# Six-channel feature groups of a tanh-attention kernel: 64 partitions of one block, or 32 partitions of two blocks

## The chip, the cores and the metric

One core of a Trainium2 chip runs the whole program. The metric is device time in microseconds; the kernel before takes 6139.32 us (median of three runs, 6136.94 to 6142.77).

## What is computed

The input x has 8 images of 128 channels and 36 x 36 positions. The reference applies a convolution layer with its own attention, and then, on each image's 1296 tokens of 128 channels, an additive (tanh) attention and a mixture-of-experts layer. The change concerns the tanh attention:

```python
q = jnp.einsum('bld,ed->ble', x, Wq) + bq
k = jnp.einsum('bld,ed->ble', x, Wk) + bk
t = jnp.tanh(q[:, :, None, :] + k[:, None, :, :])
scores = jnp.einsum('bijd,d->bij', t, w) + bw[0]
attn = jax.nn.softmax(scores, axis=-1)
return jnp.einsum('bij,bjd->bid', attn, x)
```

The term t has 8 x 1296 x 1296 x 128 elements. Everything around it runs once per image (group norm, 3 x 3 convolutions, a 1156-key softmax attention; then the gate, top 8 of 1296 tokens for each of 64 experts, two expert matmuls).

## The kernel before

**How tanh becomes matmuls.** A weighted sum of tanh over a small group of channels is one quotient. With a pattern s of signs for the group's channels, the sum of w tanh(q + k) is N / D, where D adds exp(s.q) exp(s.k) over all patterns, and N adds the same products, each times c_s = s.w. Both are inner products over patterns, so a matmul that contracts over the patterns gives N or D for a tile of 128 keys by 432 queries. A group of five channels has 32 patterns and a group of six has 64. The 128 channels are 16 groups of five (80 channels) and 8 groups of six (48).

**Feature blocks.** The patterns of all groups fill NF = 8 blocks of 128 partitions: blocks 0 to 3 hold four groups of five each, 32 partitions a group; blocks 4 to 7 hold two groups of six each, 64 partitions a group. The sign matrix is built by `signs` (lines 522 to 537) with GpSimd's affine selects. From it come the key features `kf` (128 partitions, 8 blocks, 128 keys; made once per image by `keys`, stored in HBM, fetched by `prefetch`) and the query features `qf` (one tile per block: part 0 is exp, for D; part 1 is part 0 times c_s, for N; made by `query_block`: a matmul, an ACT exponential, a GpSimd multiply). All data are float32, and each float32 matmul stands in the trace as two loads and two matmuls.

**Loops.** For each of the 8 images, three chunks of 432 queries; for each chunk, 11 tiles of keys, ten of 128 and one of the last 16. A pair of chunk and key tile is a unit. A unit of 128 keys has 12 slots (line 49), in each of which two groups are worked on, h = 0 and 1, each in a PSUM bank of its own. The slots go in rounds of three: two groups of five in one half (64 partitions) of a block, two in the other half, then the two groups of six of a block. The half that is taken first alternates from round to round. The unit of the last 16 keys has two slots, with 32 columns of output per group and four groups in a bank (lines 65 to 67, 952 to 955). There are 240 units of 12 slots and 24 of two: 2928 slots.

**A slot on the engines** (main loop, lines 1113 to 1146). For slot p, TensorE computes n, the numerators of slot p (`numerators`, into the pool `ps_n` of four banks), and d, the denominators of slot p + 3 (`denominators`, LAG = 3, into the pool `ps_d`, two buffers of two banks). ACT takes the logarithm of d (line 972), and every second slot exponentiates the negative of two slots' logarithms (line 975), which gives 1 / D. DVE multiplies n by it. In the rounds' first two slots the products go to `rp` (line 1003) and GpSimd adds them up (lines 1010, 1012). In the third slots (k = 2, 5, 8, 11, DVE_PAIRS) DVE multiplies in PSUM and adds to `accd` itself: two multiplies at line 997 and two adds at line 999; at k = 2, the unit's first, it multiplies one half straight into `accd` at line 992, then lines 993 and 994.

**Side work.** The next image's convolutions and attention, its keys, the weighted sums of the finished chunk and the gate are generators in four lanes. After a slot's own work, `matmul_turn` (line 1077) lets them put one burst of matmuls on TensorE, paced by a balance that is counted when the program is built, not in DVE_PAIRS' preceding slots except for the lane `first_of_all`. Their PSUM tiles come from the same four banks as n. `take_turns` (line 1072) lets them issue the other engines' work. Everything is issued in the order in which it is written (a manual schedule); each engine takes its own instructions in that order.

**Query blocks of the next chunk.** `qf` has nine buffers for eight blocks. In a chunk's last unit, a block of the next chunk is made when one of the present chunk's is no longer needed; IN_TURN gives the order of blocks, and lines 1136 to 1141 choose the slots.

Of the kernel before, what the change touches and what calls it, by code (L numbers as in the profile page):

```python
# [3 lines left out]

# [6 lines left out]
F32 = mybir.dt.float32  # L11
# [9 lines left out]
CH = 432  # L21
# [24 lines left out]
NF = 8  # L46
# [1 line left out]

SLOTS = []
for m in range(NF // 2):  # L50
    for i in range(2):
        half = (m + i) % 2
        SLOTS.append((m, [slice(64 * half + 32 * h, 64 * half + 32 * h + 32) for h in range(2)]))
    SLOTS.append((NF // 2 + m, [slice(64 * h, 64 * h + 64) for h in range(2)]))
NP = len(SLOTS)
IN_TURN = [m + i for m in range(NF // 2) for i in (0, NF // 2)]
LAG = 3
SHIFT = 6.5
DVE_PAIRS = (2, 5, 8, 11)
# [2 lines left out]


HALVES = [slice(0, 64), slice(64, 128)]
REM_BANKS = [[(q + i, rows) for i in range(2) for rows in HALVES] for q in (0, 2)]
REM_BANKS.append([(NF // 2 + i, slice(0, 128)) for i in range(4)])
REM_SLOTS = [REM_BANKS[:2], REM_BANKS[2:]]


@with_exitstack  # L70
def kernel(
# [58 lines left out]
    with ExitStack() as loop, ExitStack() as score:  # L130
# [82 lines left out]
            pattern=[[C // G, G], [0, C // G]], channel_multiplier=-1,  # L213
        )

        pairs = const.tile([128, 2, 2], F32, tag="pairs", name="pairs")
        nc.gpsimd.memset(pairs, 0.0)
        for s in range(2):
            nc.gpsimd.memset(pairs[64 * s : 64 * s + 64, 1, s : s + 1], 1.0)
            for o in (32 * s, 64 + 32 * s):  # L220
                nc.gpsimd.memset(pairs[o : o + 32, 0, s : s + 1], 1.0)

        by_key = const.tile([128, 2, REM], F32, tag="by_key", name="by_key")
        for s in range(2):
# [297 lines left out]
        def signs():  # L522

            sign = big_tile("sign")[:, : NF * 128]
            nc.gpsimd.memset(sign, 0.0)
            for n, first, half in ((5, 0, sign[:, : NF * 64]), (6, FIVES, sign[:, NF * 64 :])):
                groups = NF * 64 >> n
                for r in range(n):
                    v = half.rearrange("p (g h b l) -> p g h b l", g=groups, b=2, l=2**r)
                    for bit, value in ((0, -1.0), (1, 1.0)):  # L530
                        w = v[:, :, :, bit, :]
                        nc.gpsimd.affine_select(
                            out=w, in_=w, compare_op=ALU.not_equal, fill=value, base=-first - r,
                            pattern=[[-n, groups], [0, 2 ** (n - 1 - r)], [0, 2**r]],
                            channel_multiplier=1,
                        )
            return sign

        feat = {}
# [127 lines left out]
        def keys(b, tiles):  # L667

            xT = prepared[b][1]
            yield matmuls(1)  # L670
            for t in tiles:
                o, n = KT[t]
                first = (b, t) == (0, order[0])
                if first:
                    kf_of[0] = kfp.tile([128, NF, 128], F32, tag="kf", name="kf")
                for q0 in (0, NF // 2):
                    some = slice(q0, q0 + NF // 2)
                    pk = aux("pk1").rearrange("p (q t) -> p q t", t=128)
                    for q in range(NF // 2):
                        bmm(pk[:, q, :n], a_k[:, (q0 + q) * 128 : (q0 + q + 1) * 128],  # L680
                           xT[:, o : o + n], start=True, stop=True)
                    yield TAKE
                    if first:
                        ks = kf_of[0][:, some, :]
                    else:
                        ks = kstp.tile([128, NF // 2, 128], F32, tag="ks", name="ks")
                    nc.scalar.activation(ks[:, :, :n], pk[:, :, :n], AF.Exp)
                    kd3 = kd[b][t].rearrange("p (q t) -> p q t", t=128)[:, some, :]
                    if n == REM:

                        for x in range(2):
                            nc.gpsimd.tensor_scalar(
                                ks[:, :, (x + 1) * n : (x + 2) * n], ks[:, :, :n],
                                pairs[:, min(q0, 1), x : x + 1], None, ALU.mult,
                            )
                        nc.sync.dma_start(kd3[:, :, : 2 * n], ks[:, :, n : 3 * n])
                    else:
                        nc.sync.dma_start(kd3, ks)
                    if q0 > 0:
                        made.add((b, t))  # L700
                    yield matmuls()
# [209 lines left out]
        def drain(*gens):  # L911
            for g in gens:
                for _ in g:
                    pass
# [22 lines left out]
        def new_block(b, c, q):  # L937
            qf = qfp.tile([128, 2, CH], F32, tag="qf", name="qf")
            qf_of[b, c, q] = qf
            return query_block(b, c, q, qf)  # L940

        def products(u, k, part, outs):

            b, c, j = units[u]
            kf = kf_of[u]
            if j < NKT - 1:
                q, rows = SLOTS[k]
                for h in range(2):
                    mm(outs[h][:, :CH], kf[rows[h], q, :], qf_of[b, c, q][rows[h], part, :],  # L949
                       start=True, stop=True)  # L950
                return
            for out, bank in zip(outs, REM_SLOTS[k]):
                for i, (q, rows) in enumerate(bank):
                    mm(out[32 * i : 32 * i + 32, :CH], kf[rows, q, :32],  # L954
                       qf_of[b, c, q][rows, part, :], start=True, stop=True)

        def banks(u, k):
            return 2 if units[u][2] < NKT - 1 else len(REM_SLOTS[k])

        def denominators(p):  # L960

            if p >= len(slots):
                return
            u, k = slots[p]
            d = ps_d.tile([128, 2, 512], F32, tag="d", name="d")
            n = banks(u, k)
            products(u, k, 0, [d[:, h, :] for h in range(n)])
            if k % 2 == 0:
                lq_of[u, k // 2] = lp.tile([128, 4, CH], F32, tag="lq", name="lq")
            lq = lq_of[u, k // 2]  # L970
            o = 2 * (k % 2)
            nc.scalar.activation(lq[:, o : o + n, :], d[:, :n, :CH], AF.Ln)  # L972
            if k % 2 == 1:
                some = lq[:, : o + n, :]
                nc.scalar.activation(some, some, AF.Exp, scale=-1.0)  # L975

        def numerators(p):
            ns = [ps_n.tile([128, 512], F32, tag="n", name="n") for _ in range(banks(*slots[p]))]
            products(*slots[p], 1, ns)
            return [ps[:, :CH] for ps in ns]  # L980

        def terms(p, ns):

# [116 lines left out]
        a_q, a_k, cs_s, fb_s, eb_s = (feat[n] for n in ("a_q", "a_k", "cs_s", "fb_s", "eb_s"))  # L1100
        drain(tokens(0), keys(0, order[:1]))
        for i, q in enumerate(IN_TURN):
            if i < 3:
                drain(new_block(0, 0, q))
            else:
                first_of_all.append(new_block(0, 0, q))
        for p in range(LAG):
            denominators(p)
        drain(keys(0, order[1:3]))
        prefetch(1)  # L1110
        urgent.append(keys(0, order[3:]))
# [1 line left out]
        for p, (u, k) in enumerate(slots):  # L1113
            b, c, j = units[u]
            rem = j == NKT - 1
            if k == 0:
                prefetch(u + 2)
                if c == 0 and j == 1:
                    if b > 0:
                        gates.append(gating(b - 1))  # L1120
                    if b == NB - 1:
                        gates.append(residuals(4))
                    if b + 1 < NB:
                        background.extend(
                            (normal(b + 1), conv_keys(b + 1), layer0(b + 1), tokens(b + 1),
                             keys(b + 1, range(NKT)))
                        )
            take_turns(p, k)
            ns = numerators(p)
            denominators(p + LAG)  # L1130
            terms(p, ns)
            if pending and pending[0][0] <= p:
                exps(p, *pending.popleft()[1:])
            last = p + 1 == len(slots) or slots[p + 1][0] != u

            if j == order[-1] and u + 1 < len(units) and k % 3:
                used = IN_TURN.index(SLOTS[k][0]) + 1
                if used < NF:
                    first_of_all.append(new_block(*units[u + 1][:2], IN_TURN[used]))
            elif j == order[-2] and last and u + 2 < len(units):  # L1140
                first_of_all.append(new_block(*units[u + 2][:2], IN_TURN[0]))
            matmul_turn(p, k)
            if last and rem:
                first_of_all.append(rem_scores(p, u, live.pop("rem")))
            elif last:
                pending.append((p + 7, u, sums(u)))
# [211 lines left out]
```

The softmax here doesn't subtract the row's maximum and nothing guards it: scores larger than these inputs give would overflow.

## Time and profile before

| | |
|---|---|
| median of the runs | 6139.32 us |
| profiled execution, its span | 6139.0 us |
| mean granted TensorE clock | 0.985 of full speed |
| ACT busy between 400 and 6000 us | 5020 us of 5600 |
| DVE busy between 400 and 6000 us | 4509 us of 5600 |
| numerator matmuls, L949, 32 rows | 7680 instructions, 571 ns |
| numerator matmuls, L949, 64 rows | 3840 instructions, 580 ns |
| denominator matmuls, L949, 32 rows | 7680 instructions, 575 ns |
| denominator matmuls, L949, 64 rows | 3840 instructions, 534 ns |
| last-key matmuls, L954, 64 rows | 384 + 384 instructions, 528 ns |
| last-key matmuls, L954, 128 rows | 192 + 192 instructions, 538 ns |
| ACT logarithm, L972 | 2904 of 881 ns, 24 shorter |
| ACT exponential, L975 | 1440 of 1644 ns, 24 shorter |
| DVE multiply to rp, L1003 | 3912 of 600 ns |
| DVE multiply in PSUM, L997 | 1440 of 608 ns |
| DVE add to accd, L999 | 1440 of 602 ns |

The profile is of one execution, and its rows are groups of like instructions: line, engine, how often, mean time of one. PE is TensorE's matmuls, PEld its weight loads, which overlap them. "32*128" is a matmul with 32 rows of contraction and 128 columns of output. Matmuls overlap and their ends are modelled, so their busy times can't be added up to a span; the starts in the timeline tell more. An idle time is followed by "<-" and the instruction that ended it.

### The profile page before, as it was taken

Reading aid. Unit: us, or ns where it says so; the run is one execution under the profiler, and the core shown is the slowest. Engines: PE = TensorE matmul, PEld = TensorE weight load, DVE = VectorE, ACT = ScalarE, POOL = GpSimd, SP = SyncE. Lnnn points to the kernel's source line nnn. Section 1 sums busy time; section 2 is a strip of 40 time slices with the busy share of each in tenths; the row PEclk is TensorE's granted clock in tenths of the full one; section 3 lists DMA queues with packets and bytes.
Section 4 is the critical chain, followed back from the end, with each engine's and each line's share of the span. In section 5 each row is a group of like instructions: output and inputs, shape, how many; then the busy total and the mean of one; then the engine's idle time right before and its main releaser. Section 6 shows DMA issues by size and latency. Waiting matters only on the chain.

```text
span 6139.0 us, 93072 instructions
## 1 busy us (share of the span) xinstructions
PE 5957.9 (97%) x33480; PEld 2862.1 (47%) x33480; DVE 4796.4 (78%) x9521; ACT 5279.9 (86%) x5371; POOL 4597.7 (75%) x2819
## 2 busy tenths in 40 slices
PE   7999999999999999999999999999999999999996
PEld 5454444544544445444455444454444544544443
DVE  4787878877788787877888777887778877788882
ACT  1888898888988888889998889888898888999990
POOL 4777777777787777778778786877777777787870
PEclk9999999999999999999999999999999999999997
DMA  1210011100110002100111001110011100110008
GB/s 44 70 37 22 25 62 38 34 25 28 68 43 20 26 27 71 39 24 23 44 55 39 22 24 59 44 39 22 20 65 40 34 25 28 58 50 29 28 20 297
DMA packets 151519, 270.87 MB, mean 44 GB/s; under 512 B 45648, under 2 KB 76752, under 8 KB 151056
## 3 DMA queue, kind: packets, MB, share of 16 engines
q1 hardware_dynamic: 151056, 264.92, 13.0%
q8 instruction: 264, 4.33, 0.3%
q14 instruction: 199, 1.63, 0.1%
HBM read 200.41 MB, written 64.19 MB: 43 GB/s over the span
## 4 chain that ended last, share of the span: by engine, by line
PE 77%; ACT 7%; DVE 6%; issue 6%; POOL 2%; DMA 1%; SPq 0%; DVEq 0%; POOLq 0%; ACTq 0%
PE n L949 37%; PE d L949 12%; PE pa L284 7%; PE pc L284 5%; ACT lq L972 5%; PE s L284 3%; PE pk L284 3%; PE pq L284 3%; DVE rp L1003 2%; DVE n L997 1%; DVE accd L999 1%; PE d L954 1%; ACT lq L975 1%; DMA w<-in_weight_dram 1%; PE n L954 1%
## 5 line engine op out<-in xcount | busy, mean ns | idle before, releaser
L1012 POOL TENSOR_TENSOR accp<-accp,rp 128x864 f32<-128x864 f32 x1440 | 2915.8, 2025 | 1041.0 <-DVE rp L1003 948.8
L949 PE MATMUL n<-qf,kf 32*128 32x432 f32 (+1 forms) x11520 | 3325.3, 574 | 46.5 <-ACT e L1032 13.3
L949 PE MATMUL d<-qf,kf 32*128 32x432 f32 (+1 forms) x11520 | 2991.6, 561 | 38.7 <-ACT lq L972 38.2
L972 ACT ACTIVATE lq<-d 128x864 f32<-128x864 f32 x2928 | 2524.2, 878 | 542.6 <-PE d L949 512.1
L1003 DVE TENSOR_TENSOR rp<-n,lq 128x432 f32<-128x432 f32 x3912 | 2173.3, 600 | 743.5 <-PE d L949 542.8
L975 ACT ACTIVATE lq<-lq 128x1728 f32<-128x1728 f32 (+1 forms) x1464 | 2398.2, 1638 | 46.3
L949 PEld LDWEIGHTS n<-qf,kf 32*128 32x128 f32 (+1 forms) x11520 | 1206.4, 184 | 1600.3 <-DVE rp L1003 581.5
L949 PEld LDWEIGHTS d<-qf,kf 32*128 32x128 f32 (+1 forms) x11520 | 1090.0, 185 | 422.1 <-issue 224.7
L997 DVE TENSOR_TENSOR n<-n,lq 128x432 f32<-128x432 f32 x1440 | 814.9, 608 | 142.1 <-PE n L949 88.5
L999 DVE TENSOR_TENSOR accd<-n,accd 128x432 f32<-128x432 f32 x1440 | 866.3, 602 | 24.6
L1010 POOL TENSOR_TENSOR accp<-rp 128x864 f32<-128x864 f32 x240 | 485.2, 2022 | 197.7 <-DVE rp L1003 195.6
L711 POOL TENSOR_SCALAR qf<-qf,cs_s 128x432 f32<-128x432 f32 x192 | 260.9, 1365 | 45.0 <-ACT qf L710 44.4
L284 PEld LDWEIGHTS pa<-xh,e 128*108 128x108 f32 x1920 | 222.5, 174 | 131.1 <-DVE rp L1003 56.0
L1021 POOL TENSOR_TENSOR accd<-accp,accd 128x432 f32<-128x432 f32 x240 | 265.2, 1105 | 18.8
L1019 POOL TENSOR_TENSOR accp<-accp 128x432 f32<-128x432 f32 x240 | 264.4, 1102 | 16.7
L284 PE MATMUL pa<-xh,e 128*108 128x129 f32 x1920 | 262.9, 283 | 8.7 <-ACT e L1032 5.2
L284 PE MATMUL s<-q,k 128*116 128x432 f32 x480 | 230.3, 568 | 1.7 <-DVE q L316 1.4
L284 PEld LDWEIGHTS pk<-xT,a_k 128*128 128x128 f32 x1408 | 171.2, 192 | 107.0 <-DVE n L997 33.7
L462 POOL TENSOR_TENSOR tot<-tot,e 116x432 f32<-116x432 f32 x192 | 212.0, 1104 | 6.0 <-ACT e L471 4.6
L471 ACT ACTIVATE e<-s 116x432 f32<-116x432 f32 x240 | 124.9, 520 | 98.3 <-PE s L284 97.9
L284 PE MATMUL pa<-e,vw 116*128 116x432 f32 x480 | 204.6, 549 | 0.0
L284 PE MATMUL pk<-xT,a_k 128*128 128x128 f32 (+1 forms) x1408 | 202.5, 287 | 0.1
(213 smaller groups left out, 3788.4 us busy)
## 6 DMA issues: line engine op xcount, KB each, us to landing
kf<-kd SPq DMA_DIRECT2D x239, 512.0 KB
kd<-ks SPq DMA_DIRECT2D x158, 256.0 KB
w<-in_weight_dram SPq DMA_DIRECT2D x32, 1024.0 KB
wk_t<-wk_t_d SPq DMA_DIRECT2D x7, 768.0 KB
wv_t<-wv_t_d SPq DMA_DIRECT2D x7, 768.0 KB
wq_t<-wq_t_d SPq DMA_DIRECT2D x7, 768.0 KB
x<-in_x_dram SPq DMA_DIRECT2D x8, 648.0 KB
t<-tokd SPq DMA_DIRECT2D x96, 54.0 KB
```

The source lines that it names most:

```text
L284: mm(out, lhsT, rhs, **kw)
L711: nc.gpsimd.tensor_scalar(qf[:, 1, :], qf[:, 0, :], cs_s[:, q : q + 1], None, ALU.mult)
L949: mm(outs[h][:, :CH], kf[rows[h], q, :], qf_of[b, c, q][rows[h], part, :], start=True, stop=True)
L972: nc.scalar.activation(lq[:, o : o + n, :], d[:, :n, :CH], AF.Ln)
L975: nc.scalar.activation(some, some, AF.Exp, scale=-1.0)
L997: mult(ns[h], ns[h], lq[:, o + h, :])
L999: nc.vector.tensor_add(live["d"], ns[h], live["d"])
L1003: mult(rp[:, h, :], n, lq[:, o + h, :])
L1010: nc.gpsimd.tensor_add(live["p"], live["r"], rp)
L1012: nc.gpsimd.tensor_add(live["p"], live["p"], rp)
L1019: nc.gpsimd.tensor_add(s[:, 0, :], s[:, 0, :], s[:, 1, :])
L1021: nc.gpsimd.tensor_add(d, s[:, 0, :], d)
```

## The change

The groups of six are laid out anew. Their 64 patterns no longer stand on 64 partitions of one block: the 32 patterns of the first five signs stand on 32 partitions of block 4 or 5 with the sixth sign negative, and on the same partitions of block 6 or 7 with the sixth sign positive. A block of 4 to 7 so holds 32 patterns of four groups. A slot of groups of six takes, for each of its two groups, two 32-row matmuls, over block 4 + m // 2 and block 6 + m // 2, which accumulate in the group's PSUM bank; all slots now work on one half of the partitions, and the half alternates from slot to slot.

`products` becomes a generator that yields after each block, and `in_rounds` takes turns between the numerators of slot p and the denominators of slot p + 3: n and d of the first block, then n and d of the second. For groups of five this leaves the order of issue as it was. The slots of the last 16 keys take eight accumulating 64-row matmuls where they had four of 128 rows. The order of the query blocks and the slots at which the next chunk's are made (NEXT_AT) follow the new order of use; four of the first chunk's blocks, not three, are made ahead of the loop. `signs` has 32 affine selects where it had 22, and `pairs`, the mask for the last keys' features, loses the form for 64 partitions.

```diff
 for m in range(NF // 2):
-    for i in range(2):
-        half = (m + i) % 2
-        SLOTS.append((m, [slice(64 * half + 32 * h, 64 * half + 32 * h + 32) for h in range(2)]))
-    SLOTS.append((NF // 2 + m, [slice(64 * h, 64 * h + 64) for h in range(2)]))
+    for blocks, half in (
+        ((m,), m % 2),
+        ((m,), (m + 1) % 2),
+        ((NF // 2 + m // 2, NF // 2 + 2 + m // 2), m % 2),
+    ):
+        rows = [slice(64 * half + 32 * h, 64 * half + 32 * h + 32) for h in range(2)]
+        SLOTS.append((blocks, rows))
-IN_TURN = [m + i for m in range(NF // 2) for i in (0, NF // 2)]
+IN_TURN = [0, 4, 6, 1, 2, 3, 5, 7]
+NEXT_AT = {1: 4, 5: 6, 6: 1, 7: 2, 8: 3, 10: 5, 11: 7}
...
-REM_BANKS = [[(q + i, rows) for i in range(2) for rows in HALVES] for q in (0, 2)]
-REM_BANKS.append([(NF // 2 + i, slice(0, 128)) for i in range(4)])
+REM_BANKS = [[((q + i,), rows) for i in range(2) for rows in HALVES] for q in (0, 2)]
+REM_BANKS.append([
+    ((NF // 2 + m, NF // 2 + 2 + m), rows) for m in range(2) for rows in HALVES
+])
...
-            for n, first, half in ((5, 0, sign[:, : NF * 64]), (6, FIVES, sign[:, NF * 64 :])):
-                groups = NF * 64 >> n
-                for r in range(n):
...
+            for n, first, groups, top in ((5, 0, 16, None), (6, FIVES, 8, -1.0), (6, FIVES, 8, 1.0)):
+                part = sign[:, at - NF * 64 : at - NF * 64 + groups * 32]
+                at += groups * 32
+                for r in range(5):
...
+                if top is not None:
+                    filled(part.rearrange("p (g l) -> p g l", g=groups), top, first + 5,
+                           [[-n, groups], [0, 32]])
...
-                q, rows = SLOTS[k]
-                for h in range(2):
-                    mm(outs[h][:, :CH], kf[rows[h], q, :], qf_of[b, c, q][rows[h], part, :],
-                       start=True, stop=True)
+                blocks, rows = SLOTS[k]
+                for q in blocks:
+                    for h in range(2):
+                        mm(outs[h][:, :CH], kf[rows[h], q, :],
+                           qf_of[b, c, q][rows[h], part, :],
+                           start=(q == blocks[0]), stop=(q == blocks[-1]))
+                    yield
                 return
             for out, bank in zip(outs, REM_SLOTS[k]):
-                for i, (q, rows) in enumerate(bank):
-                    mm(out[32 * i : 32 * i + 32, :CH], kf[rows, q, :32],
-                       qf_of[b, c, q][rows, part, :], start=True, stop=True)
+                for i, (blocks, rows) in enumerate(bank):
+                    for q in blocks:
+                        mm(out[32 * i : 32 * i + 32, :CH], kf[rows, q, :32],
+                           qf_of[b, c, q][rows, part, :],
+                           start=(q == blocks[0]), stop=(q == blocks[-1]))
+            yield
...
+        def in_rounds(*gens):
+            for _ in zip_longest(*gens):
+                pass
...
-            if i < 3:
+            if i < 4:
                 drain(new_block(0, 0, q))
...
-            ns = numerators(p)
-            denominators(p + LAG)
-            terms(p, ns)
+            ns = []
+            in_rounds(numerators(p, ns), denominators(p + LAG))
+            terms(p, [ps[:, :CH] for ps in ns])
...
-            if j == order[-1] and u + 1 < len(units) and k % 3:
-                used = IN_TURN.index(SLOTS[k][0]) + 1
-                if used < NF:
-                    first_of_all.append(new_block(*units[u + 1][:2], IN_TURN[used]))
+            if j == order[-1] and u + 1 < len(units) and k in NEXT_AT:
+                first_of_all.append(new_block(*units[u + 1][:2], NEXT_AT[k]))
```

More of the change, by code (lines that the diff above doesn't have):

```diff
@@ L2 @@
 from contextlib import ExitStack
-from itertools import chain
+from itertools import chain, zip_longest
 import concourse.bass as bass
@@ L214 @@
         )
-        pairs = const.tile([128, 2, 2], F32, tag="pairs", name="pairs")
+        pairs = const.tile([128, 2], F32, tag="pairs", name="pairs")
         nc.gpsimd.memset(pairs, 0.0)
         for s in range(2):
-            nc.gpsimd.memset(pairs[64 * s : 64 * s + 64, 1, s : s + 1], 1.0)
             for o in (32 * s, 64 + 32 * s):
-                nc.gpsimd.memset(pairs[o : o + 32, 0, s : s + 1], 1.0)
+                nc.gpsimd.memset(pairs[o : o + 32, s : s + 1], 1.0)
         by_key = const.tile([128, 2, REM], F32, tag="by_key", name="by_key")
@@ L525, in signs, with filled @@
             nc.gpsimd.memset(sign, 0.0)
-            for n, first, half in ((5, 0, sign[:, : NF * 64]), (6, FIVES, sign[:, NF * 64 :])):
-                groups = NF * 64 >> n
-                for r in range(n):
-                    v = half.rearrange("p (g h b l) -> p g h b l", g=groups, b=2, l=2**r)
-                    for bit, value in ((0, -1.0), (1, 1.0)):
[L531 to L536, printed above, removed]
+            def filled(w, value, first, pattern):
+                nc.gpsimd.affine_select(
+                    out=w, in_=w, compare_op=ALU.not_equal, fill=value, base=-first,
+                    pattern=pattern, channel_multiplier=1,
+                )
+            at = NF * 64
+            for n, first, groups, top in ((5, 0, 16, None), (6, FIVES, 8, -1.0), (6, FIVES, 8, 1.0)):
+                part = sign[:, at - NF * 64 : at - NF * 64 + groups * 32]
+                at += groups * 32
+                for r in range(5):
+                    v = part.rearrange("p (g h b l) -> p g h b l", g=groups, b=2, l=2**r)
+                    for bit, value in ((0, -1.0), (1, 1.0)):
+                        filled(v[:, :, :, bit, :], value, first + r,
+                               [[-n, groups], [0, 2 ** (4 - r)], [0, 2**r]])
+                if top is not None:
+                    filled(part.rearrange("p (g l) -> p g l", g=groups), top, first + 5,
+                           [[-n, groups], [0, 32]])
             return sign
@@ L693, in keys @@
                                 ks[:, :, (x + 1) * n : (x + 2) * n], ks[:, :, :n],
-                                pairs[:, min(q0, 1), x : x + 1], None, ALU.mult,
+                                pairs[:, x : x + 1], None, ALU.mult,
                             )
@@ L966, in denominators @@
             n = banks(u, k)
-            products(u, k, 0, [d[:, h, :] for h in range(n)])
+            yield from products(u, k, 0, [d[:, h, :] for h in range(n)])
             if k % 2 == 0:
@@ L975, in denominators, with numerators @@
                 nc.scalar.activation(some, some, AF.Exp, scale=-1.0)
[L977 to L980, printed above, removed]
+        def numerators(p, ns):
+            for _ in range(banks(*slots[p])):
+                ns.append(ps_n.tile([128, 512], F32, tag="n", name="n"))
+            yield from products(*slots[p], 1, ns)
+        def in_rounds(*gens):
+            for _ in zip_longest(*gens):
+                pass
         def terms(p, ns):
@@ L1107 @@
         for p in range(LAG):
-            denominators(p)
+            drain(denominators(p))
         drain(keys(0, order[1:3]))
```

## The prediction

> **What bounds the kernel now.** I read the page's engine shares and its chain of waits first, then the costliest groups, then one stretch of the timeline.
>
> ```profile
> PE 5957.9 (97%) x33480; PEld 2862.1 (47%) x33480; DVE 4796.4 (78%) x9521; ACT 5279.9 (86%) x5371; POOL 4597.7 (75%) x2819
> ...
> PE 77%; ACT 7%; DVE 6%; issue 6%; POOL 2%; DMA 1%; SPq 0%; DVEq 0%; POOLq 0%; ACTq 0%
> ```
>
> TensorE sets the end, but ACT is close behind, and a busy TensorE is not a TensorE that streams. The timeline (start, length, instruction, count) shows one round of three slots; k counts the slots of a unit:
>
> ```profile
> 2018.55 0.63 PE L949 MATMUL n<-qf,kf 32*128 32x432 f32 x2
> ...
> 2018.57 0.63 PE L949 MATMUL d<-qf,kf 32*128 32x432 f32 x2
> ...
> 2019.49 0.30 PEld L949 LDWEIGHTS n<-qf,kf 64*128 64x128 f32 x4 [0.62 <-DVE q L314]
> 2019.49 1.00 PE L949 MATMUL n<-qf,kf 64*128 64x432 f32 x4
> 2019.68 1.12 DVE L1003 TENSOR_TENSOR rp<-n,lq 128x432 f32<-128x432 f32 x2 [0.34 <-PE d L949]
> ...
> 2019.96 0.19 PEld L949 LDWEIGHTS d<-qf,kf 64*128 64x128 f32 x2 [0.17 <-issue]
> 2020.32 0.89 PE L949 MATMUL d<-qf,kf 64*128 64x432 f32 x4
> 2020.32 0.19 PEld L949 LDWEIGHTS d<-qf,kf 64*128 64x128 f32 x2 [0.17 <-issue]
> ...
> 2020.72 1.12 DVE L997 TENSOR_TENSOR n<-n,lq 128x432 f32<-128x432 f32 x2
> ...
> 2021.14 1.36 PE L284 MATMUL pc<-xwin,wq_t 128*128 128x216 f32 x6
> 2021.75 1.24 DVE L999 TENSOR_TENSOR accd<-n,accd 128x432 f32<-128x432 f32 x2
> ...
> 2022.43 0.19 PEld L949 LDWEIGHTS n<-qf,kf 32*128 32x128 f32 x2 [0.27 <-DVE accd L999]
> 2022.43 0.63 PE L949 MATMUL n<-qf,kf 32*128 32x432 f32 x2
> ...
> 2022.90 0.53 PE L949 MATMUL n<-qf,kf 32*128 32x432 f32 x2
> ...
> 2023.28 0.52 PE L949 MATMUL n<-qf,kf 32*128 32x432 f32 x1
> ```
>
> Each float32 product is two passes; a pass of 432 columns takes 0.36 us (the loads of d at 2019.96 and 2020.32). In a 32-row slot n of this slot and d of the slot three ahead lie on opposite halves, so four tiles stream at once: 2 passes, 0.72 us, and 0.94 from 2018.55 to 2019.49. In a 64-row slot n takes the whole array for two passes, then d: 4 passes, 1.44, and 1.65 to 2021.14. The 0.2 over is a change of shape (drain 0.09, a weight load in the open 0.11). Where a 32-row slot follows another, 2022.43 to 2023.28, only the load shows.
>
> The last thing to see is [0.27 <-DVE accd L999]: n of the next slot needs a PSUM bank that L999 has only just let go. The four n banks go round with the side work's, so after a side burst the second matmul of the next slot takes the bank of the 64-row slot's first n. Of the 946 rounds of three slots that lie within 12 us of the next, 725 have a side burst after the 64-row slot; where one also stands after the round's first slot, and none after its second, the next slot starts 0.04 us (median) after that release. TensorE and DVE are level there.
>
> **The change part by part.**
>
> *Switches removed.* Between 400 and 6000 us the TensorE records hold 786 direct steps from 32 to 64 rows and 260 back; the rest has a side burst between, which keeps its switches. 1046 x 0.2 = 209 us less TensorE time, if nothing else waits. ACT would allow it: in that window it is busy 5020 of 5600 us.
>
> *Passes.* A six-channel slot becomes two rounds, each with n and d on four tiles: 2 x 2 passes, 1.44 as before, if four tiles stream at 0.36. They do: passes start at 2022.54 (after the load), 2022.90 and 2023.28. The doubled instructions are issued 7 ns apart (starts of n and d, 2018.55 and 2018.57, with four tiles in 0.02). Cost 0. Against this stands the Trainium skill, "TensorE: Matmul & The Clock Gate", Part 3, whose table gives four row tiles a measured speed-up of 3.07, not 4. By it, as an estimate, a pass would take 0.36 x 4/3.07 = 0.47 and the change would cost 960 x 4 x 0.11 = 422 us more. The rows show no such loss, and the sum goes by them.
>
> *n comes later.* This decides. Take k1's end of streaming, 2019.38, as zero. Before: switch 0.2, two passes 0.72, 0.16 until the record's end: n is ready at 1.08. After: no switch, but n shares its slot with d and needs four passes: 1.44 + 0.16 = 1.60. It is 0.52 later, while TensorE is 0.2 earlier. Behind it on DVE stand L997 twice and L999 twice; the first bank is free 1.63 after L997 starts (2020.72 to 2022.35). In the rows above, L997 waits for rp until 2020.72, so it moves to about 2021.00, the release to 2022.64, and the next slot's second matmul from 2022.43 to about 2022.69: 0.26 lost, switch already counted. TensorE is in order, so d of that slot, and ACT, follow.
>
> Over the trace, per round (delay of L997 = 0.52 less the time DVE was busy past n; slack = start of the next matmul less the release; change = the later of "release" and "TensorE 0.2 earlier", no 0.2 where a side burst stands before the 64-row slot):
> - 192 of the 725 are the unit's first, where L992 frees the bank at once: slack 1.25 at the mean, gain 23.
> - 270 of the other 533 start within 0.12 of the release: mean delay 0.35, +96.
> - 217 have slack, 0.72 at the mean: +22.
> - 46 start before it and depend on another bank: 0.
>
> Sum +95, between -145 (0.2 kept in all 725) and 725 x 0.52 = +377. Of the 221 rounds without a burst after the 64-row slot, 66 have one after the next slot, whose bank is then that one: 66 x 0.41 = 27 or 0; I take 13. 129 have none at all and take 4.6 us where ACT needs 3 x 0.881 + 1.5 x 1.644 = 5.1: ACT's, 0.
>
> *n behind d's wait.* n of the second block is now queued behind d of the first. In 24% of the 64-row slots L972 frees d's bank only after the slot's start, by 0.56 at the mean; before, n's 0.8 us covered that. 960 x 0.24 x 0.56 = 130 at most, 0 at least; such stretches are ACT's own already, so a quarter: 33.
>
> *The last keys' slots (L954).* Four 128-row matmuls become eight of 64 rows on four tiles, half the array.
>
> ```profile
> 2003.40 1.65 PE L954 MATMUL n<-qf,kf 64*32 64x432 f32 x16
> ...
> 2006.83 0.93 PE L954 MATMUL n<-qf,kf 128*32 128x432 f32 x8
> ```
>
> Sixteen 64-row instructions take four passes, eight of 128 rows two: +0.72, for n and d, in 24 units: 48 x 0.72 = 35. It is all TensorE there: ACT idles 3.27 us. Least 0. At most, if a tile's four passes are not overtaken, each tile starts with the fourth pass of the one before: 13 passes against 2, 48 x 3.96 = 190. The passes of h0 are overtaken by h1's in the rows above, so 35.
>
> *Small things.* Of `sign`, 12 fills keep 256 columns (22 took 23.5 us) and 20 have 128; at half, +0.6, at full length +11; TensorE waited for it (5.7 us). A fourth block ahead of the loop: 0.6 each on TensorE and ACT. Together 2. The next chunk's blocks come at other slots, four in a row: POOL then has 2 x 2.03 + 4 x 1.365 = 9.5 us in four slots of 2.0 (a round's mean is 5.98), 1.5 late in 23 chunks, 0 to 35; needed some five slots later, so 0. DMAs: none added or moved.
>
> *Given back.* A later TensorE waits less for ACT (weight loads of d waited 146 us for L972): a quarter of 95 + 13, -27; between 0 and -108.
>
> Sum: 95 + 13 + 33 + 35 + 2 - 27 = +151. The profiled execution is 6139.0, the median 6139.3, so nothing is converted: **6290 us**.
>
> **Rivals.**
> *The switches win* (0.22). DVE is idle a fifth of the loop and may catch up before the bank matters. For: ACT idles 512 us for d of L949, which now comes 0.2 sooner. Against: the 0.04. All kept: 6139 - 209 + 37 = 5967; half of it, 6070, is more likely. It decides if the waits for DVE come to less than some 170 us in all.
> *ACT gates n* (0.15): the full 130, nothing given back: 6290 + 97 + 27 = 6414. For: two d banks only. Against: ACT has 10% idle.
> *They cancel* (0.06): 6139, within 0.2%, which is about what a measurement of this kernel tells from none.
> *It doesn't do what it says* (0.02): n and d of a six-channel slot go one after the other, 960 x 1.44 = 1382 more, 7521. Against: the four-tile rows.
>
> **How the numbers follow.** The forecast has 0.55, its own range is 6180 to 6430: the low end with all 108 given back and no ACT part, the high end with 27 instead of 13, 130 instead of 33, nothing back. The range reaches down to 6100, into the first rival, and up to 6450; about 0.2 is outside. Faster 0.22; same 0.06; slower 0.55 + 0.15 + 0.02 = 0.72.
>
> **What would show it.** L949 has 32-row forms alone, 15360 each of n and d, and no direct switch is left. Six-channel slots that run at 1.44 to 1.5 prove the passes. L997's idle time for n (88.5 us) should grow to some 300, TensorE's loads of n should wait longer for accd, and ACT should idle more for d. If L997 starts no later after k1's end than 1.35, or the bank is free before TensorE wants it, the forecast is wrong and the kernel faster; if TensorE waits for L972 in the middle of slots, ACT gates it.

## The result and the profile after

The changed kernel takes 6373.35 us (median of four runs, 6368.98 to 6380.27) against 6138.3 for the kernel before, run beside it: ratio 1.0384, 95% interval 1.0369 to 1.0399. It is slower by 235 us, on the side and inside the range that were forecast, and 83 us above the forecast.

The page of the changed kernel, with the engines' shares and the chain of waits:

```profile
PE 6151.7 (96%) x41544; PEld 3203.8 (50%) x41544; DVE 4825.0 (76%) x9521; ACT 5302.8 (83%) x5371; POOL 4604.8 (72%) x2827
...
PE 81%; DVE 6%; issue 5%; ACT 5%; POOL 2%; DMA 1%; SPq 0%; DVEq 0%; POOLq 0%; ACTq 0%
```

DVE, ACT and GpSimd do the work that they did before, to within 30 us each, in a span that is 239.5 us longer; their shares fall. The extra time is waiting. The groups by shape say who waits (line, engine, tiles, count, busy time, mean ns, then idle time before and its enders; L962 is L949 of before, L990 is L972, L1019 is L997, L1014 is L992):

```profile
L962 PE MATMUL n<-qf,kf 32*128 32x432 f32 x15360 | 4125.9, 556 | 64.5 <-DVE accd L1021 21.3 <-ACT e L1054 10.3 <-DVE rp L1025 10.1
L962 PE MATMUL d<-qf,kf 32*128 32x432 f32 x15360 | 3463.3, 563 | 28.5 <-ACT lq L990 25.2
L990 ACT ACTIVATE lq<-d 128x864 f32<-128x864 f32 x2904 | 2523.9, 882 | 729.2 <-PE d L962 705.2 <-PE n L962 9.2 <-PE d L970 2.1
...
L1019 DVE TENSOR_TENSOR n<-n,lq 128x432 f32<-128x432 f32 x1440 | 821.6, 611 | 413.0 <-PE n L962 209.9 <-ACT lq L993 62.8 <-ACT lq L990 49.0
...
L1014 DVE TENSOR_TENSOR accd<-n,lq 128x432 f32<-128x432 f32 x240 | 145.8, 607 | 171.4 <-PE n L962 117.2 <-PE d L962 22.0 <-ACT lq L993 18.3
```

All slots have 32 rows now. DVE waits for n at the six-channel slots' first multiply for 209.9 us where it was 88.5, and at the first multiply of a unit's first such slot (L1014) for 117.2 where it was 19.2; ACT waits for d for 705.2 us where it was 512.1. The waiting that TensorE itself does hardly stands in the matmuls' rows; it shows in the weight loads. The list of waits of the kernel before (who waited for whom, us in total, times, longest):

```profile
PEld n L949 <- DVE rp L1003: 581.5, 1032, 1.5
...
ACT lq L972 <- PE d L949: 512.1, 665, 3.3
...
PEld n L949 <- DVE accd L999: 198.5, 472, 1.6
...
PEld d L949 <- ACT lq L972: 146.1, 199, 5.0
...
DVE n L997 <- PE n L949: 88.5, 111, 1.2
...
DVE accd L992 <- PE n L949: 19.2, 27, 1.3
```

And of the changed kernel:

```profile
PEld n L962 <- DVE rp L1025: 400.2, 1048, 1.6
...
PEld n L962 <- DVE accd L1021: 318.1, 665, 2.0
...
PEld d L962 <- ACT lq L990: 115.6, 154, 5.0
```

The loads of n wait less for the products of the first two slots (400.2 us for 581.5) and more for the third slot's adds (318.1 for 198.5): the waits have moved to the instructions behind the late n.

One round of the changed kernel, second and third slot, in the timeline (weight loads and other engines left out where not needed):

```profile
2100.76 0.63 PE L962 MATMUL n<-qf,kf 32*128 32x432 f32 x2
...
2101.17 0.37 DVE L319 TENSOR_TENSOR q<-q,pc 128x216 f32<-128x216 f32 x1
...
2101.61 0.68 PE L962 MATMUL n<-qf,kf 32*128 32x432 f32 x2
2101.61 0.23 PEld L962 LDWEIGHTS n<-qf,kf 32*128 32x128 f32 x2 [0.18 <-issue]
2101.70 0.19 PEld L962 LDWEIGHTS d<-qf,kf 32*128 32x128 f32 x2
...
2101.97 0.68 PE L962 MATMUL n<-qf,kf 32*128 32x432 f32 x2
...
2102.33 0.68 PE L962 MATMUL n<-qf,kf 32*128 32x432 f32 x2
...
2102.70 0.68 PE L962 MATMUL n<-qf,kf 32*128 32x432 f32 x2
...
2102.89 0.53 PE L962 MATMUL d<-qf,kf 32*128 32x432 f32 x2
2103.25 0.62 DVE L1019 TENSOR_TENSOR n<-n,lq 128x432 f32<-128x432 f32 x1 [0.24 <-PE n L962]
2103.35 0.30 PEld L289 LDWEIGHTS pc<-xwin,wq_t 128*128 128x128 f32 x2 [0.62 <-DVE rp L1025]
```

Two things are to be seen. The four passes stand 0.36 us apart, so four tiles do stream at full rate, and DVE waits for n and starts only when all four are done, at 2103.25. And the removed switch has brought nothing in this round: from the second slot's first matmul to the side burst is 2103.35 - 2100.76 = 2.59 us, and in the round shown of before it is 2021.14 - 2018.55 = 2.59. The first n streams at 2101.61, with no switch. The other three tiles' loads come only at 2101.66 and later, in the open: by the order of the ring of four, the second n takes the bank of the side burst before, which DVE finished reading (L319) at 2101.54. Before, the switch stood over that wait. The same shows over the 515 rounds of the changed kernel that have a burst after the first and the third slot and none between (500 before). At the median, the third slot's first matmul comes 0.09 us sooner after the start of the second slot's last pass (0.37 for 0.46); but the slot's second n starts 0.23 after the first, where it was 0.11, and its last pass, of n or d, 1.45 after the first, where it was 1.37.

**The granted clock.** The trace also has TensorE's granted clock, which is either full or 0.5 in these traces. In the changed kernel's trace a matmul of the main loop takes 922 ns at the median where it is 0.5, and 521 where it is full. In the main loop, from its first matmul to the start of the last unit, it is 0.5 for 88.7 us before and 136.5 in the changed kernel. A round is counted here from its first n to the next round's. The 912 rounds at full clock in both traces are 201 us longer together, the 47 others 31. So the loss is not the clock's in the main.

### The profile page after: what moved, and what is told of

Its sections match the earlier page's. It is cut to its first block, busy times and chain, and to the rows that moved or that the text cites. A ratio compares the mean times of both kernels' runs of the same rounds, so it can differ in the third digit from the quotient of the medians.

```text
span 6378.5 us, 110485 instructions
## 1 busy us (share of the span) xinstructions
PE 6151.7 (96%) x41544; PEld 3203.8 (50%) x41544; DVE 4825.0 (76%) x9521; ACT 5302.8 (83%) x5371; POOL 4604.8 (72%) x2827
## 4 chain that ended last, share of the span: by engine, by line
PE 81%; DVE 6%; issue 5%; ACT 5%; POOL 2%; DMA 1%; SPq 0%; DVEq 0%; POOLq 0%; ACTq 0%
PE n L962 45%; PE d L962 9%; PE pa L289 7%; PE pc L289 5%; PE s L289 3%; ACT lq L990 3%; PE pk L289 3%; PE pq L289 2%; DVE n L1019 2%; DVE accd L1021 1%; PE d L970 1%; PE n L970 1%; DVE rp L1025 1%; POOL accp L1034 1%; DMA w<-in_weight_dram 1%
## 5 line engine op out<-in xcount | busy, mean ns | idle before, releaser
L962 PE MATMUL n<-qf,kf 32*128 32x432 f32 x15360 | 4125.9, 556 | 64.5 <-DVE accd L1021 21.3
L962 PE MATMUL d<-qf,kf 32*128 32x432 f32 x15360 | 3463.3, 563 | 28.5 <-ACT lq L990 25.2
L990 ACT ACTIVATE lq<-d 128x864 f32<-128x864 f32 x2928 | 2536.5, 880 | 753.1 <-PE d L962 705.2
L962 PEld LDWEIGHTS n<-qf,kf 32*128 32x128 f32 x15360 | 1860.8, 185 | 1606.7 <-DVE rp L1025 400.2
L962 PEld LDWEIGHTS d<-qf,kf 32*128 32x128 f32 x15360 | 1269.6, 185 | 241.2 <-ACT lq L990 115.6
L1019 DVE TENSOR_TENSOR n<-n,lq 128x432 f32<-128x432 f32 x1440 | 821.6, 611 | 413.0 <-PE n L962 209.9
L1021 DVE TENSOR_TENSOR accd<-n,accd 128x432 f32<-128x432 f32 x1440 | 867.2, 602 | 24.7
L1014 DVE TENSOR_TENSOR accd<-n,lq 128x432 f32<-128x432 f32 x240 | 145.8, 607 | 171.4 <-PE n L962 117.2
```

The source lines that it names most:

```text
L1019: mult(ns[h], ns[h], lq[:, o + h, :])
L1021: nc.vector.tensor_add(live["d"], ns[h], live["d"])
```

## The experiments

Each ran beside the kernel before on its chip, in rounds of three unless said; ratios are to the kernel before, with their 95% intervals.

**d ahead of n in the kernel before.** A dose of late n with no other part of the change.

```diff
-            ns = numerators(p)
-            denominators(p + LAG)
+            six = k % 3 == 2 and not rem
+            if six:
+                denominators(p + LAG)
+            ns = numerators(p)
+            if not six:
+                denominators(p + LAG)
```

> The kernel before with d issued ahead of n in the 64-row slots alone: n there is 0.72 us later, nothing else changes (no switch is removed, no instruction added). Bank theory: slower by 150 to 350 us, 6290 to 6490, as a dose of the same kind. Rival (loads, last keys' slots, ACT): within 20 of 6138, or faster, since d comes 0.72 sooner for ACT.

6415.22 us, 1.0453 (1.0437 to 1.0468): 280 us slower, with 64-row slots, every switch and every instruction as before. The waits of this kernel:

```profile
DVE n L997 <- PE n L949: 497.1, 635, 7.0
...
DVE accd L992 <- PE n L949: 155.2, 208, 2.6
```

DVE's waits for n grow as in the changed kernel and further. The dose is not pure: n now also stands behind d's wait for ACT. It shows that n's place in these slots can cost more than the whole loss.

**The changed kernel with n early again.** The second block's numerators are left out; d keeps its four passes and so does the slot.

```diff
                 blocks, rows = SLOTS[k]
+                if part == 1:
+                    blocks = blocks[:1]
```

> The changed kernel with the second block's numerator matmuls of the six-channel slots left out (half of those groups' numerators is missing from the output). d still takes four passes, so a slot is as long and has as few switches, but n is ready 0.72 us sooner. Bank theory: the whole loss comes back and the removed switches show, 5960 to 6100, below the kernel before. Rival, the loss lies in the slots' own length (weight loads in the open, four tiles that do not stream at full rate) or in ACT: 6300 to 6375.

6195.76 us, 1.0092 (1.0077 to 1.0108). 178 of the 235 us come back, but not the rest: the removed switches should then have shown, and the kernel is still 58 us above the one before. What is left of DVE's wait for n at the multiply of L1019 (here L1021) is less than in the kernel before, 88.5:

```profile
DVE n L1021 <- PE n L964: 38.4, 45, 1.3
```

**The control: d short, n late.** As many matmuls are left out, on the other side: d takes the first block alone, n takes the first block twice.

```diff
                 blocks, rows = SLOTS[k]
-                for q in blocks:
+                if len(blocks) == 2:
+                    blocks = blocks[:1] * (1 + part)
+                for i, q in enumerate(blocks):
                     for h in range(2):
                         mm(outs[h][:, :CH], kf[rows[h], q, :],
                            qf_of[b, c, q][rows[h], part, :],
-                           start=(q == blocks[0]), stop=(q == blocks[-1]))
+                           start=(i == 0), stop=(i == len(blocks) - 1))
```

> A control for after_n_half: the changed kernel with as many matmuls of the six-channel slots left out, but on the other side. d takes the first block alone; n takes the first block twice, so its four passes and its lateness stay (both sums of these groups are wrong). Late-n theory: n is what counts, most of the loss stays, 6290 to 6375. Rival, fewer matmuls and loads or a shorter d made after_n_half fast: about 6196 again.

6406.38 us, 1.0442 (1.0427 to 1.0458), a little above the changed kernel and above the range that late n was given. Fewer matmuls, fewer loads and an earlier d give no time at all while n is late. Nor does the clock hide a gain: it is 0.5 for 215 us of this kernel's loop and 219 of the one with n early, and over the rounds at full clock in both traces this kernel is 228 us behind the kernel before, the one with n early 12.

```profile
DVE n L1021 <- PE n L964: 227.7, 442, 5.6
DVE accd L1016 <- PE n L964: 145.1, 178, 2.8
```

DVE's waits for n are about those of the changed kernel (209.9 and 117.2). So it is n's lateness and not the number of instructions, weight loads or d.

**n of both blocks ahead of d.** Is n held up by d's wait for ACT inside the slot?

```diff
-            in_rounds(numerators(p, ns), denominators(p + LAG))
+            drain(numerators(p, ns), denominators(p + LAG))
```

> The changed kernel with n of both blocks issued ahead of d of both, so that n no longer stands behind d's wait for ACT. Rival, ACT gates n: faster by 60 to 130, 6240 to 6315. Bank theory: within 33 of 6373. If d then can't run beside n because n's four passes are not overtaken, slower by up to 960 x 0.72 = 690.

6363.45 us, 1.0369 (1.0354 to 1.0385), 10 us below the changed kernel with overlapping intervals. ACT does not gate n. That d runs beside n all the same, though queued behind all of n, shows in the trace: d's first matmul starts 0.33 us after n's first in the six-channel slots (median), and 0.30 in the changed kernel, long before n's fourth pass. So a matmul for an idle half of the array overtakes those that wait for the busy half.

**The last keys' slots alone.** The second block is left out in n and d of the last 16 keys.

```diff
                 for i, (blocks, rows) in enumerate(bank):
+                    blocks = blocks[:1]
```

> The changed kernel with the second block's matmuls left out in the last-key slots alone, n and d (the scores of the last 16 keys of each chunk are wrong). The bank of groups of six then takes two passes as before the change. If that part costs 48 x 0.72 us: 35 faster, 6325 to 6350. If tiles wait for one another (13 passes): 150 or more faster. If it hides: within 10 of 6373.

6338.53 us, 1.0330 (1.0314 to 1.0345): 35 us, the price that was worked out, all of it on the path. The two slots in the changed kernel's timeline, eight matmuls for two banks and eight for one:

```profile
2084.34 1.65 PE L970 MATMUL n<-qf,kf 64*32 64x432 f32 x16
...
2087.77 1.67 PE L970 MATMUL n<-qf,kf 64*32 64x432 f32 x16
```

The second was the 0.93 of eight 128-row instructions.

**Both parts left out**, by the two edits above together.

> The changed kernel with both parts left out: the second block's numerators in the six-channel slots, and the second block in the last-key slots. If the two costs add: 6155 to 6165, level with the kernel before or above it, so that the 1046 removed switches bring nothing that shows. If late n and the last keys hid the switches' gain: 6000 to 6120. If they overlap: 6175 to 6196.

6165.24 us, 1.0047 (1.0030 to 1.0064). The two costs add (178 + 31), and with both gone the kernel with 1046 switches less is still 29 us slower than the one with them. So the switches' 209 us were not hidden under late n. In the rounds that have a side burst after the first and the third slot and none between, the stretch from the second slot's first matmul to the third slot's last has a median of 3.08 us before, 3.08 after and 3.10 in this kernel.

Where the 29 us stand can be read from the traces. The 892 rounds at full clock in both traces are 18 us shorter together than before: that is what shows of the 209. The other 67 are 40 us longer, and 6 us stand ahead of the loop. The clock is 0.5 for 195 us of this kernel's loop, where it was 89. In the units behind the last keys it is 0.5 for 72 us, where it was none, and these units are together 17 us longer; the fourth units of the chunks are together 16 us longer, with 58 us at 0.5 for 44. No run shows whether the lower clock makes these rounds longer or comes of waits in them. The new slots of the query blocks are not the place: the chunks' last units, in which they are made, are 3 us shorter together, and the first units of all chunks 7.

**Banks freed sooner, products into SBUF.** In both kernels the third slots' products went into `lq` and not back into PSUM (at the unit's first third slot too, for h1).

```diff
                     for h in range(2):
-                        mult(ns[h], ns[h], lq[:, o + h, :])
+                        mult(lq[:, o + h, :], ns[h], lq[:, o + h, :])
                     for h in range(2):
-                        nc.vector.tensor_add(live["d"], ns[h], live["d"])
+                        nc.vector.tensor_add(live["d"], lq[:, o + h, :], live["d"])
```

> The changed kernel, but the products of the third slots go into lq in SBUF and not back into PSUM, so an n bank is free after its multiply (some 0.6 and 1.1 us after the first multiply starts) and not after the add (1.63 and 2.35). Bank theory (n of the six-channel slots is half a us later, so DVE frees its banks later and TensorE waits for them): most of the 235 us come back, 6130 to 6230, and the second matmul of the next round no longer starts right at a release. Rival, ACT gates n inside the slot, or the doubled loads and the last keys' slots cost the time: 6340 to 6375.

> The kernel before with the same edit, products into lq. Bank theory: the banks were just in time there (270 of 533 rounds started within 0.12 us of the release), so a smaller gain, 6050 to 6120. Rival (banks don't matter): 6125 to 6150.

7215.34 us, 1.1761 (1.1740 to 1.1782), and 7096.74 us, 1.1562 (1.1543 to 1.1581). Every expectation failed, and the rows of the first kernel say why:

```profile
L1021 DVE TENSOR_TENSOR accd<-lq,accd 128x432 f32<-128x432 f32 x1440 | 1794.2, 1246 | 24.8
L1019 DVE TENSOR_TENSOR lq<-n,lq 128x432 f32<-128x432 f32 x1440 | 812.5, 603 | 599.7 <-PE n L962 474.7 <-PE d L962 117.0 <-ACT lq L990 3.3
```

The adds took 602 ns with one operand in PSUM and take 1246 with both in SBUF (1440 in the kernel before). The multiplies are unchanged. This pair says nothing of the banks; it says that DVE's own time in these slots is on the path, since two slower adds a round cost 842 us in the one kernel and 958 in the other. A part of that can be the clock's: the mean granted clock is 0.932 and 0.935 in these two, and 0.981 and 0.985 without the edit.

**The first bank sooner, by order alone.** DVE multiplies and adds h0, then h1, in both kernels.

```diff
                     for h in range(2):
                         mult(ns[h], ns[h], lq[:, o + h, :])
-                    for h in range(2):
                         nc.vector.tensor_add(live["d"], ns[h], live["d"])
```

> The changed kernel with DVE's four instructions of a third slot in the order multiply h0, add h0, multiply h1, add h1. The first bank is free after two instructions, some 1.25 us after the first starts and not 1.63; the second some 2.6 and not 2.35. Bank theory: faster by 30 to 130, 6245 to 6345, as the first bank is the one that the next round's second matmul needs. Rival: within 15 of 6373; slower by 20 to 60 if the second bank counts as much.

> The kernel before with the same order on DVE. Bank theory: the banks are just in time there, so a smaller gain than in the changed kernel, 10 to 60, 6078 to 6128. Rival: within 15 of 6138.

6361.82 us, 1.0369 (1.0354 to 1.0385), 12 us below the changed kernel, and 6142.92 us, 1.0008 (0.9998 to 1.0017), no change. The gain that was expected of the first bank is not there. Summed over the rounds, the time from the first slot's start to the second's falls by 92 us against the changed kernel, and from the second's to the third's it grows by 95: the wait moves to the next bank, which is freed later in this order. This fits that DVE's whole chain of four instructions is late, and not one bank.

**Two more orders in the kernel before**, as tries at a better one. First d ahead of n in the rounds' first slots:

```diff
-            ns = numerators(p)
-            denominators(p + LAG)
+            early_d = k % 3 == 0 and not rem
+            if early_d:
+                denominators(p + LAG)
+            ns = numerators(p)
+            if not early_d:
+                denominators(p + LAG)
```

> The kernel before with d issued ahead of n in the rounds' first slots alone, where n's second matmul waits for a bank. d then doesn't stand behind that wait, and ACT gets it sooner. If TensorE's order at that wait is what late banks cost: 20 to 100 faster, 6040 to 6120. If DVE and the banks set the pace whatever d does: within 15 of 6138. If d's own wait for ACT then holds n up: slower by 10 to 60.

6195.82 us, 1.0098 (1.0083 to 1.0113). Here n is put behind d's wait for ACT, and DVE's wait for n at L1003 goes from 51.5 to 383.1 us. Then the side work's instructions behind the slot's own:

```diff
-            take_turns(p, k)
             ns = numerators(p)
             denominators(p + LAG)
             terms(p, ns)
+            take_turns(p, k)
```

> A try at a better version: the kernel before with the side work's instructions on DVE, ACT and GpSimd issued behind a slot's own and not ahead of them. n's banks come free sooner by the side work's DVE time (0.37 us an instruction in the convolutions), the side work's bank later by the slot's (1.2). If late n banks are the whole cost of waiting: 20 to 80 faster, 6056 to 6116. If the side work's bank, which stands in the same ring of four, counts as much: within 30 of 6136 or slower.

6530.52 us, 1.0637 (1.0619 to 1.0654). The side work's bank stands in the same ring and is freed later in this order, and the loads of n wait 776.2 us for L1003's products, where it was 581.5. That the side work's bank alone makes the 389 us was not tested. No kernel here beats the one before.

## Why the prediction came out as it did

**Passes: right.** Four tiles stream at 0.36 us a pass, as the row of before had it, and not at the 0.47 that the Trainium skill's packing table would make of it ("TensorE: Matmul & The Clock Gate", Part 3).

**n comes later: the mechanism is right, its size was too small.** In the rounds with bursts after the first and the third slot, the first multiply of the third slot starts 1.16 us (mean) after the second slot's n was ready before, and 1.63 after: 0.47 later, where the sum's step had 0.52 less what DVE's own work covers. The sum gave late n 95 + 13 + 33 - 27 = 114 us with everything around it; leaving the late half out gives back 178 us, and the control shows that fewer matmuls and loads do not. DVE's wait for n at the first multiply was to grow to some 300 us; it grew to 209.9, and to 117.2 at L1014.

**Where the step was mis-sized.** Each round's change was taken as the later of "release" and "TensorE 0.2 earlier", and 0.2 was credited wherever there was slack. That credit is what failed: the 0.2 is not gained in the third slot, because a bank wait stood under the switch. With the switch gone the second n meets a bank that is still held, and d's loads, queued behind it, come in the open. The sign that was named, a six-channel slot of 1.44 to 1.5, did not come: in the rows shown the slot takes 1.74 from its first matmul to the side burst (2101.61 to 2103.35), and 1.65 before (2019.49 to 2021.14). Set beside the sum's classes, with a round counted from its second slot to the next round's and at full clock in both traces: the units' first rounds with a burst behind them changed by -1 us together (187 rounds), where -23 was summed; the others with a burst by +154 (499 rounds), where it was 96 + 22; those without a burst by +11 (203 rounds), where it was 13. Whatever there was of the next two terms is in these figures too. The 209 us were rightly taken as an upper bound "if nothing else waits"; something else did, in the same slot and not in the next, where the prediction looked.

**Given back (-27): not shown.** The wait that it goes by, of d's loads for ACT, did fall, from 146.1 to 115.6 us; no run shows that this saved time. ACT's own idle time for d grew by 193 us.

**n behind d's wait (33): not there.** Issuing n first gains 10 us, with overlapping intervals.

**Last keys (35): right**, 35 measured, and 31 with n early.

**Small things (2): a little more.** The 20 shorter fills of `sign` take 681 ns each, not half of 1093, and the loop's first n stands at 167.7 us in the changed kernel's trace and 161.9 before; but it stands at 162.8 in the run with n early, which makes the same start, so this start moves by itself.

**The clock: not in the sum.** The 47 rounds in which the granted clock is 0.5 in one of the two traces are 31 us longer together, and no term stood for them. Their cause stays open.

**The rivals.** "The switches win" fell with the kernel that has both costs out. "ACT gates n" fell with n first, though its time, 6414, lay nearer to the result than the forecast's (41 us off, and 83). The forecast's reason was the right one and its bank too narrowly named: it was the first bank in the prediction, and when DVE's order freed that one sooner, the wait moved to the second.

## What to carry to other kernels

When an engine that is busy to the end also runs round a small ring of buffers, a saving on it counts only if the buffer that it takes next is already free: here 209 us of removed switches met a ring of four PSUM banks, and 18 of it showed. A result's place inside a slot is a cost of its own: the same four passes, with n done after four and not after two, cost 178 us, and a control that removes as much work from the other operand tells this from the work itself.

## What was not expected of the hardware

A DVE add of 128 x 432 with both operands in SBUF depends on GpSimd. In the changed kernel with products in `lq`, the 421 adds of L1021 during which GpSimd stood still took 607 ns at the mean; the 1019 that met a GpSimd instruction took 1510 at the mean, 3227 at most. With one operand in PSUM the same add (L1021 of the changed kernel) takes 602 beside GpSimd and 605 without. The Trainium skill says so: "A DVE instruction with two SBUF inputs contends with a GpSimd instruction that reads SBUF" ("SBUF — State Buffer", "Who interferes with whom"), and this trace agrees.
